# Moving normalisation to ScalarE, an FP4 addition to GpSimd, quantising x in pairs, and giving reads of shared banks top priority

## The chip, the core and the metric

The kernel runs on one core of a Trainium2 chip. The metric is the device time of one execution in microseconds (us). The engines are named as in the profile: PE is TensorE (PEld its weight loads), DVE is VectorE, ACT is ScalarE, POOL is GpSimd, and SP is the engine that issues the DMAs here.

## The reference

The kernel computes two layers on 16 sequences of 512 tokens with 256 channels. The change touches the first one only:

```python
# attention: 16 heads of 16 channels, each turned into a latent of 32
q, k, v = split(x @ c_attn_w.T + c_attn_b)           # in heads
q_lat = rope(q @ q2l_w.T + q2l_b);  k_lat = rope(k @ kv2l_w.T + kv2l_b)
v_lat = v @ kv2l_w.T + kv2l_b
att = softmax(causal((q_lat @ wqk_w.T + wqk_b) @ k_lat.T * 32**-0.5))
y   = (att @ v_lat) @ l2o_w.T + l2o_b
x   = layernorm(x + y @ cproj_w.T + cproj_b)
# feed-forward with FP4 values: blocks of 16 along the last axis
# fp4(t): scale = max|t| of a block / 6, round t/scale to 0, .5, 1, 1.5, 2, 3, 4, 6, times scale
h = silu(fp4(x) @ fp4(w_gate).T) * (fp4(x) @ fp4(w_up).T)   # 704 wide
x = layernorm(x + fp4(h) @ fp4(w_down).T)
# second layer: a recurrence over the 512 tokens, then a gated channel mix
```

## The kernel before

The program has two stages. The first does all of the first layer, one sequence ("batch" `b`) after the other, and stores the result to a DRAM tile `xs`. The second does the recurrence and the channel mix; it begins when the last rows of `xs` are stored, and the change leaves it as it is.

In the first stage the instructions of PE are written out by hand (`tc.manual_schedule` for PE alone), and a scheduler orders those of the other engines by priority, which follows program order unless something raises it. The hand-written order is a list of slots `(b, g, n)`: for each batch, each of four groups `g` of four heads, and each of three sets `n` of score blocks (`BLOCKS`: 512, 384, and 256 + 128 wide). In a slot PE computes the scores of four heads into four PSUM banks (`scores`, L551). DVE adds the mask, takes the row maximum and writes p to SBUF (L563, the maximum in `nm`), which frees the bank. ACT takes the exponential of p (L576), two heads later (`LAG`). One slot later PE transposes p (`turn`, L586) and ACT copies the result out of PSUM (L588, pT). When the three sets of a group are turned, PE multiplies by the values (`weighted`, L617), and `divide` (L631 to L638) divides by the row sums, whose reciprocal POOL spreads out (L602, rcx).

Beside each half slot `Beside` runs tasks from the hand-written list `PLAN`, in its order, paced by the times in `TIME`. A task is named by a letter, the batch counted from the present one, and a part:

- `H`, `V`, `L`: the heads (L383), the values (L366) and the latents of the next groups. For the latents PE multiplies twice (L401), DVE applies cosine and sine (L411, L416), POOL adds both (L417, qc and kc), PE multiplies qc by one more matrix (L420, ps_qf) and ACT copies it out (L422, qr).
- `O`: the output projection of the previous batch (L435). DVE adds the residual x (L441) and takes mean and variance (L89, L90, in mv). POOL makes rstd in two instructions (`rstd_of`: L82 ve, L84 a power). DVE subtracts and multiplies each of four tiles (L448).
- `Q`: queues the FP4 quantisation of one tile of x, 128 tokens by 256 (`fp4`).
- `U`: gate and up projections of one tile. PE transposes the quantised tile (L483, ps_xq), ACT copies it (L485), PE multiplies for both halves of 352 (L493, pg and pu), ACT takes a tanh (L498, th), DVE forms h (L499, L500), and the quantisation of h is queued.
- `D`: the down projection. PE transposes the quantised h (L514, ps_h), ACT copies it (L517 to L519, hT), PE multiplies (L524, ps_d), DVE adds the residual (L527), then `layernorm` as in O but for one tile (L96), and the store to `xs` (L530).

`fp4` is a generator of ten instructions. On DVE: block maximum and scale (L290, L291), inverse (L292, L293), the product x times inverse (L296, q), its power of two (L298), the rounding constant (L299, m), the addition q + m (L302). On POOL: q − m (L303) and the product with the scale (L304, xq or hq). Queued generators are stepped one yield per half slot (`vector_step`), and in full where their result is needed (`vector_done`).

All tiles of PSUM but one come from one pool of seven rotating banks (`mm`), so each PE instruction that opens a bank waits for the engine that read that bank seven tiles ago. The residual x of a batch is loaded at the batch's start (`load_residual`, L355, three buffers), and POOL adds the projection's bias to it (L357).

Of the kernel before, what the change touches and what calls it, by code (L numbers as in the profile page):

```python
# [10 lines left out]
F32 = mybir.dt.float32  # L11
# [46 lines left out]
def tile_kernel(ctx: ExitStack, tc: tile.TileContext, I: dict, out: bass.AP):  # L58
# [33 lines left out]
    def layernorm(dst, src):  # L92
        mv = small.tile([P, 4, 2], F32, tag="mv", name="mv")
        stats_into(mv[:, 0, :], src)
        rs = rstd_of(mv, 1, LN_EPS)
        nc.vector.tensor_scalar(dst, src, mv[:, 0, 0:1], rs[:, 0:1], ALU.subtract, ALU.mult)  # L96
# [42 lines left out]
    with ExitStack() as a:  # L139
# [119 lines left out]
        xres = a.enter_context(tc.tile_pool(name="xres", bufs=3))  # L259
# [7 lines left out]
        def mm(name):  # L267
            return ps_m.tile([P, 512], F32, tag="mm", name=name)

        def fp4(dst, x, nb, rows=P):  # L270

            n = nb * 16
            sc = ffn.tile([P, 44], F32, tag="q_sc", name="q_sc", bufs=2)[:rows, :nb]
            inv = ffn.tile([P, 44], F32, tag="q_inv", name="q_inv", bufs=2)[:rows, :nb]  # L280
            q = ffn.tile([P, FF], F32, tag="q_q", name="q_q", bufs=2)[:rows, :n]
            m = ffn.tile([P, FF], F32, tag="q_m", name="q_m", bufs=2)[:rows, :n]

            def blocks(t):
# [8 lines left out]
            nc.vector.tensor_scalar(inv, inv, 1.0 - 2.0**-23, None, ALU.mult)  # L293
            if n > C:
                yield
            nc.vector.tensor_tensor(blocks(q), blocks(x), over(inv), ALU.mult)  # L296
            yield
            nc.vector.tensor_scalar(m.bitcast(U32), q.bitcast(U32), 0x7F800000, None, ALU.bitwise_and)  # L298
            nc.vector.tensor_scalar(m, m, 1.0, 1.5 * 2.0**22, ALU.max, ALU.mult)  # L299
            if n > C:  # L300
                yield
            nc.vector.tensor_tensor(q, q, m, ALU.add)  # L302
            nc.gpsimd.tensor_tensor(q, q, m, ALU.subtract)  # L303
            nc.gpsimd.tensor_tensor(blocks(dst), blocks(q), over(sc), ALU.mult)  # L304
# [55 lines left out]
        def values(b):  # L360
            v = vpad[b % 2]
            for j in range(0, NT, 2):
                ps = mm("ps_v")
                for i in range(2):
                    for cc in range(2):
                        nc.tensor.matmul(  # L366
                            ps[:, i * C : i * C + C],
                            xT_of[b][:, cc, (j + i) * P : (j + i) * P + P], wv[:, cc, :],
                            start=cc == 0, stop=cc == 1,
                        )  # L370
                for odd in range(2):
                    nc.scalar.copy(
                        v[:, j : j + 2, odd::2, odd * 16 : odd * 16 + 16],
                        ps.rearrange("p (j n o d) -> p j n o d", j=2, o=2, d=16)[:, :, :, odd, :],
                    )
                yield 0.9

        def heads(b):
            hs = heads_of[b] = att.tile([P, 4, T], F32, tag="heads", name="heads")
            for n in range(4):  # L380
                ps = mm("ps_h")
                for cc in range(2):
                    nc.tensor.matmul(  # L383
                        ps, wqk[:, cc, n, :], xT_of[b][:, cc, :], start=cc == 0, stop=cc == 1
                    )
                bias = col("cab", n) if n < 2 else cabk[:, n - 2 : n - 1]
                nc.scalar.activation(hs[:, n, :], ps, AF.Identity, bias=bias)
                yield 1.7

        def latents(b, g):  # L390
# [17 lines left out]
            for k, ps in pair(""):  # L408
                of[k] = att.tile([P, T], F32, tag=f"{k}c", name=f"{k}c", bufs=1 if k == "q" else 3)
                bias = col("q2lb" if k == "q" else "kv2lb")  # L410
                nc.vector.scalar_tensor_tensor(of[k], ps, bias, cos, ALU.add, ALU.mult)  # L411
            yield 0.86
            for k, ps in pair("s"):
                x = att.tile([P, T], F32, tag=f"{k}s", name=f"{k}s")
                bias = q2lbs if k == "q" else col("kv2lbs")
                nc.vector.scalar_tensor_tensor(x, ps, bias, sin, ALU.add, ALU.mult)  # L416
                nc.gpsimd.tensor_tensor(of[k], of[k], x, ALU.add)  # L417
# [4 lines left out]
            nc.scalar.activation(qr, ps, AF.Identity, bias=wqkb)  # L422
# [3 lines left out]
        def out_projection(b):  # L426
# [4 lines left out]
            for j in range(0, NT, 2):  # L431
# [9 lines left out]
                nc.vector.tensor_tensor(both, ps, both, ALU.add)  # L441
# [4 lines left out]
            rs = rstd_of(mv, 4, LN_EPS)  # L446
            for j in range(NT):
                nc.vector.tensor_scalar(  # L448
                    x[:, j, :], x[:, j, :], mv[:, j, 0:1], rs[:, j : j + 1],
                    ALU.subtract, ALU.mult,  # L450
                )
# [21 lines left out]
        def quantize(b, j):  # L473
            xq_of[b, j] = xq = ffn.tile([P, C], F32, tag="xq", name="xq", bufs=2)
            queue(("x", b, j), fp4(xq, x_of[b][:, j, :], C // 16))
            yield 0.0

        def ffn_up(b, j):
            vector_done(("x", b, j))
            xq = xq_of.pop((b, j))  # L480
# [4 lines left out]
            nc.scalar.copy(xqT.rearrange("p c t -> p (c t)"), ps[:, : 2 * P])  # L485
            yield 0.3
            h = ffn.tile([P, FF], F32, tag="h", name="h", bufs=2)
            for f in range(2):
# [9 lines left out]
                nc.scalar.activation(th, pg[:, :352], AF.Tanh, scale=0.5)  # L498
                nc.vector.scalar_tensor_tensor(th, th, 1.0, pg[:, :352], ALU.add, ALU.mult)  # L499
                nc.vector.scalar_tensor_tensor(h[:, fs], th, 0.5, pu[:, :352], ALU.mult, ALU.mult)  # L500
# [5 lines left out]
        def ffn_down(b, j):  # L506
# [10 lines left out]
            nc.scalar.copy(hT[:, 0:4, :].rearrange("p k t -> p (k t)"), pa)  # L517
            nc.scalar.copy(hT[:, 4, :], pb[:, :P])
            nc.scalar.copy(hT[:64, 5, :], pb[:64, P : 2 * P])  # L519
# [7 lines left out]
            nc.vector.tensor_tensor(x, ps[:, :C], x, ALU.add)  # L527
            layernorm(x, x)
# [14 lines left out]
        def scores(b, g, n):  # L543
# [14 lines left out]
            for h in range(4):  # L558
                p = pp.tile([P, T], F32, tag="p", name="p")
                nm = small.tile([P, 2], F32, tag="nm", name="nm", bufs=10)  # L560
                for u, (i, at) in enumerate(BLOCKS[n]):
                    own = slice(at, at + (i + 1) * P)
                    nc.vector.tensor_tensor_reduce(  # L563
                        out=p[:, own], in0=S[h][:, own], in1=mask[:, T - (i + 1) * P :],
# [17 lines left out]
        def turn(n, p):  # L582
# [5 lines left out]
            nc.scalar.copy(pT[:, :w], ps[:, :w])  # L588
# [35 lines left out]
        def divide():  # L624

            for b, g, py, rcx in undivided:
# [6 lines left out]
                nc.scalar.copy(rT.rearrange("p c t -> p (c t)"), ps[:, : 2 * P])  # L633
                to = y_of[b][g % 2 * 64 : g % 2 * 64 + 64, g // 2, :]
                to = to.rearrange("p (i t) -> p i t", t=P)
                for half, blocks in enumerate((slice(0, 4, 3), slice(1, 3))):
                    hs = slice(half * 64, half * 64 + 64)
                    nc.vector.tensor_tensor(to[:, blocks, :], py[hs], rT[hs], ALU.mult)  # L638
# [16 lines left out]
            "L0.1", "U-2.3", "L0.1", "U-2.3", "D-2.2", "L0.1", *["O-1"] * 2, "Q-1.0", "Q-1.1", "D-2.2",  # L655
# [48 lines left out]
        with tc.manual_schedule(engines={mybir.EngineType.PE}):  # L704
            load(0)
            load_residual(0)
# [6 lines left out]
            for slot in slots + [None]:  # L713
                if slot:
                    b, g, n = slot
                    if g == 0 and n == 0:
# [4 lines left out]
                        if b > 0:  # L721
                            load_residual(b)
                        beside = Beside(b)
                        if b == 2:
                            ta, wb, wc, bout = recurrent_weights()
                    tiles = scores(b, g, n)
# [463 lines left out]
```

## Time and profile before

| | |
|---|---|
| time, median of three runs | 2796.65 us (2793.94 to 2797.45) |
| the profiled execution's own time | 2794.07 us |
| its span | 2792.3 us |
| mean granted TensorE clock | 0.972 |
| first stage | to about 2013 us; one batch every 116.7 us when steady |
| busy in the span | PE 2542.9, DVE 1907.0, ACT 1620.5, POOL 1037.7 us |

The span is the time from the first to the last recorded event of the profiled execution. Busy time is summed per engine; the engines work side by side. In the lists of waits a line reads: waiting engine, tile and line, then the engine, tile and line that ended the wait, then total us, times and the longest. In a timeline a line reads: start and duration in us, engine, line, operation, output and inputs, form, count, and in brackets the idle time before it with what ended it.

### The profile page before, as it was taken

What the parts mean: (1) busy time and instruction counts of PE and PEld (TensorE: products, weight loads), DVE (VectorE), ACT (ScalarE), POOL (GpSimd) and SP (SyncE); (2) the same over time, 40 slices, a digit from 0 to 9 for tenths busy, and PEclk for the clock granted to TensorE, in tenths of its full rate; (3) what the DMA queues carried; (4) which work ended last, traced back from release to release, by engine and by line L of the source; (5) the groups of instructions that cost most, each with busy time, mean ns of one, the idle gap of its engine ahead of it and who ended that gap; (6) DMA issues with size and microseconds to landing.
All of it is one profiled execution on the core that took longest, in us unless ns stands there. A gap on an engine that the chain in (4) does not pass through costs nothing. (4 is left out here: it accounts for less than half of the span.)

```text
span 2792.3 us, 73881 instructions
## 1 busy us (share of the span) xinstructions
PE 2542.9 (91%) x28766; PEld 1734.2 (62%) x28766; DVE 1907.0 (68%) x5613; ACT 1620.5 (58%) x5604; POOL 1037.7 (37%) x1617
## 2 busy tenths in 40 slices
PE   6779999999999999999999999987699999999997
PEld 3445565665665666656566656555477777777775
DVE  3666777777777777777777777776636666666655
ACT  2646556665665656656566565654156666666663
POOL 3222323333332323323233232332355555555553
PEclk9879999999999999999999999999889999999999
DMA  3000000000000000000000000000011111111100
GB/s 114 24 6 11 14 13 13 14 20 14 13 12 14 20 9 18 12 14 20 7 20 13 12 14 5 14 5 7 24 34 37 37 37 37 37 37 37 37 26 24
DMA packets 58000, 61.31 MB, mean 22 GB/s; under 512 B 7857, under 2 KB 53041, under 8 KB 57650
## 3 DMA queue, kind: packets, MB, share of 16 engines
q1 hardware_dynamic: 56786, 55.54, 6.4%
q8 instruction: 226, 3.70, 0.5%
q14 instruction: 124, 1.02, 0.1%
q10 hardware_dynamic: 864, 1.05, 0.1%
HBM read 39.79 MB, written 16.78 MB: 20 GB/s over the span
## 5 line engine op out<-in xcount | busy, mean ns | idle before, releaser
L576 ACT ACTIVATE p<-p,nm 128x512 f32<-128x512 f32 (+3 forms) x1024 | 567.7, 558 | 573.7 <-DVE nm L563 571.4
L992 ACT ACTIVATE hist<-u 64x64 f32<-64x64 f32 x2048 | 444.1, 218 | 279.8 <-PE u L984 187.5
L563 DVE CUSTOM_DVE_ANT_0 p<-S,mask 128x512 f32<-128x512 f32 (+3 forms) x1024 | 441.2, 482 | 123.3 <-PE S L551 123.2
L586 PEld LDWEIGHTS ps_pt<-ident,p 128*128 128x128 f32 x2560 | 290.1, 142 | 298.5 <-DVE nm L563 100.1
L303 POOL TENSOR_TENSOR q_q<-q_q,q_m 128x256 f32<-128x256 f32 (+1 forms) x142 | 168.1, 1184 | 781.6 <-DVE q_q L302 758.8
L586 PE MATMUL ps_pt<-ident,p 128*128 128x128 f32 x2560 | 403.7, 284 | 45.4 <-DVE nm L563 37.9
L984 PEld LDWEIGHTS u<-hist,ta 128*64 128x64 f32 x8176 | 360.7, 138 | 123.2 <-ACT hist L992 50.2
L588 ACT COPY pT<-ps_pt 128x384 f32<-128x384 f32 (+1 forms) x768 | 370.3, 511 | 110.4 <-PE ps_pt L586 108.2
L984 PE MATMUL u<-hist,ta 128*64 128x32 f32 x8176 | 391.9, 219 | 11.4 <-ACT hist L992 9.9
L551 PE MATMUL S<-kc,qr 32*128 32x512 f32 (+3 forms) x2048 | 258.5, 478 | 3.1 <-ACT qr L422 0.9
L946 PE MATMUL u<-xt,wb 128*64 128x64 f32 x4128 | 224.9, 231 | 1.0 <-DVE xt L798 0.7
L82 POOL TENSOR_SCALAR ve<-mv 128x1 f32<-128x1 f32 (+2 forms) x144 | 28.4, 197 | 501.6 <-DVE mv L90 497.9
L576 ACT ACTIVATION_READ_ACCUMULATOR p<-p,nm 128x1 f32 x1024 | 196.9, 192 | 0.0
L524 PE MATMUL ps_d<-wdT,hT 128*128 128x256 f32 (+1 forms) x768 | 192.9, 393 | 2.3 <-ACT hT L517 1.3
L493 PE MATMUL pg<-wgT,xqT 128*128 128x352 f32 x512 | 182.0, 479 | 5.8 <-ACT xqT L485 5.7
L493 PE MATMUL pu<-wuT,xqT 128*128 128x352 f32 x512 | 175.6, 466 | 1.4 <-DVE nm L563 1.4
L946 PEld LDWEIGHTS u<-xt,wb 128*64 128x64 f32 x4128 | 166.6, 140 | 6.7 <-DVE xt L798 1.0
L551 PEld LDWEIGHTS S<-kc,qr 32*128 32x128 f32 x2048 | 122.7, 187 | 75.9 <-issue 36.1
L617 PE MATMUL py<-pT,vpad 128*32 128x128 f32 x5120 | 162.1, 279 | 3.4 <-ACT pT L588 3.4
L524 PEld LDWEIGHTS ps_d<-wdT,hT 128*128 128x128 f32 (+1 forms) x768 | 137.4, 192 | 43.2 <-issue 21.4
L617 PEld LDWEIGHTS py<-pT,vpad 128*32 128x32 f32 x5120 | 140.9, 112 | 36.4 <-issue 27.4
L417 POOL TENSOR_TENSOR qc<-qc,qs 128x512 f32<-128x512 f32 x64 | 81.6, 1275 | 212.0 <-DVE qs L416 211.9
(163 smaller groups left out, 4601.2 us busy)
## 6 DMA issues: line engine op xcount, KB each, us to landing
xT<-in_xT_dram SPq DMA_DIRECT2D x16, 512.0 KB
x<-in_x_dram SPq DMA_DIRECT2D x16, 512.0 KB
xs<-x SPq DMA_DIRECT2D x64, 128.0 KB
x<-xs SPq DMA_DIRECT2D x32, 256.0 KB
xm<-xs SPq DMA_DIRECT2D x32, 256.0 KB
out_dram<-o SPq DMA_DIRECT2D x64, 128.0 KB
caw<-in_caw_dram SPq DMA_DIRECT2D x1, 768.0 KB
w<-in_w_down_dram SPq DMA_DIRECT2D x2, 352.0 KB
```

What stands on the lines that cost most here:

```text
L303: nc.gpsimd.tensor_tensor(q, q, m, ALU.subtract)
L493: nc.tensor.matmul(dst[:, :352], xqT[:, cc, :], w[:, cc, fs], start=cc == 0, stop=cc == 1)
L524: nc.tensor.matmul(ps[:, :C], hT[:n, kb, :], wdT[:n, kb, :], start=kb == 0, stop=kb == NFB - 1)
L551: nc.tensor.matmul(S[h][:, at : at + w], q[rs, i * P : i * P + P], k[rs, :w], start=True, stop=True,)
L563: nc.vector.tensor_tensor_reduce(out=p[:, own], in0=S[h][:, own], in1=mask[:, T - (i + 1) * P :], scale=1.0, scalar=-MASKED, op0=ALU.add, ...
L576: nc.scalar.activation(p[:, own], p[:, own], AF.Exp, bias=nm[:, u : u + 1], scale=-1.0, accum_out=sum_of[b, g][:, cb, half, h : h + 1],)
L586: nc.tensor.transpose(ps[:, at : at + P], p[:, at : at + P], ident)
L588: nc.scalar.copy(pT[:, :w], ps[:, :w])
L617: nc.tensor.matmul(py[q * 32 : q * 32 + 32, PLACE[i][1], :], vpad[b % 2][:, j, g * 4 + h, :], pt, start=j == 0 and h % 2 == 0, stop=j == i ...
L946: nc.tensor.matmul(u[rs, k, par:n:2, bs : bs + 16], wb[:, g * 2 + k, par, half, rs], xt[:, g, at : at + n - par : 2, :], start=par == 0 an ...
L984: nc.tensor.matmul(into[cs, :, c, :], ta[:, t % 2, g * 2 + k, cs], own[:, :, c, :], start=False, stop=True, skip_group_check=True,)
L992: nc.scalar.activation(state[g][rs, :, r * 32 : r * 32 + 32].rearrange("p k (s b) -> p k s b", s=2), u[rs, :, t - t0, :] .rearrange("p k ( ...
```

## The change

Five things are changed, all in the first stage.

1. `soon` wraps an instruction in `tc.high_priority()`. It is put around the ACT and DVE instructions that read PSUM banks (and the two additions of L417 on POOL). The exponentials, which read SBUF, keep their ordinary priority.
2. Normalisation goes from DVE to ACT. POOL computes, after rstd, off = −mean × rstd in two more small instructions, and ACT applies x × rstd + off as one Identity activation for each tile (`normal`).
3. In `fp4`, the addition q + m goes from DVE to POOL where the row is longer than 512, that is for h and w_down (704).
4. x is quantised two tiles at a time, as rows of 512; `PLAN` loses Q-1.1 and Q-1.3, and the `xq` tiles are twice as long.
5. The residual is loaded at the batch's last group (`g == 3`) and has two buffers.

```diff
-    def layernorm(dst, src):
-        mv = small.tile([P, 4, 2], F32, tag="mv", name="mv")
-        stats_into(mv[:, 0, :], src)
-        rs = rstd_of(mv, 1, LN_EPS)
-        nc.vector.tensor_scalar(dst, src, mv[:, 0, 0:1], rs[:, 0:1], ALU.subtract, ALU.mult)
+    def normal(xs, mv):
+        n = len(xs)
+        rs = rstd_of(mv, n, LN_EPS)
+        off = small.tile([P, 4], F32, tag="off", name="off")
+        nc.gpsimd.tensor_tensor(off[:, :n], mv[:, :n, 0], rs[:, :n], ALU.mult)
+        nc.gpsimd.tensor_scalar(off[:, :n], off[:, :n], -1.0, None, ALU.mult)
+        for i, x in enumerate(xs):
+            nc.scalar.activation(
+                x, x, AF.Identity, bias=off[:, i : i + 1], scale=rs[:, i : i + 1]
+            )
...
-        xres = a.enter_context(tc.tile_pool(name="xres", bufs=3))
+        xres = a.enter_context(tc.tile_pool(name="xres", bufs=2))
...
+        def soon(op, *args, **kw):
+            with tc.high_priority():
+                op(*args, **kw)
...
             nc.vector.tensor_scalar(m, m, 1.0, 1.5 * 2.0**22, ALU.max, ALU.mult)
-            if n > C:
+            if n > 2 * C:
+                nc.gpsimd.tensor_tensor(q, q, m, ALU.add)
+            else:
                 yield
-            nc.vector.tensor_tensor(q, q, m, ALU.add)
+                nc.vector.tensor_tensor(q, q, m, ALU.add)
             nc.gpsimd.tensor_tensor(q, q, m, ALU.subtract)
             nc.gpsimd.tensor_tensor(blocks(dst), blocks(q), over(sc), ALU.mult)
...
-                nc.vector.scalar_tensor_tensor(x, ps, bias, sin, ALU.add, ALU.mult)
-                nc.gpsimd.tensor_tensor(of[k], of[k], x, ALU.add)
+                soon(nc.vector.scalar_tensor_tensor, x, ps, bias, sin, ALU.add, ALU.mult)
+                soon(nc.gpsimd.tensor_tensor, of[k], of[k], x, ALU.add)
...
-            rs = rstd_of(mv, 4, LN_EPS)
-            for j in range(NT):
-                nc.vector.tensor_scalar(
-                    x[:, j, :], x[:, j, :], mv[:, j, 0:1], rs[:, j : j + 1],
-                    ALU.subtract, ALU.mult,
-                )
+            normal([x[:, j, :] for j in range(NT)], mv)
...
         def quantize(b, j):
-            xq_of[b, j] = xq = ffn.tile([P, C], F32, tag="xq", name="xq", bufs=2)
-            queue(("x", b, j), fp4(xq, x_of[b][:, j, :], C // 16))
+            xq_of[b, j] = xq = ffn.tile([P, 2 * C], F32, tag="xq", name="xq", bufs=2)
+            both = x_of[b][:, j : j + 2, :].rearrange("p j c -> p (j c)")
+            queue(("x", b, j), fp4(xq, both, C // 8))
             yield 0.0
 
         def ffn_up(b, j):
-            vector_done(("x", b, j))
-            xq = xq_of.pop((b, j))
+            vector_done(("x", b, j // 2 * 2))
+            xq = xq_of[b, j // 2 * 2][:, j % 2 * C : j % 2 * C + C]
...
-                nc.scalar.activation(th, pg[:, :352], AF.Tanh, scale=0.5)
-                nc.vector.scalar_tensor_tensor(th, th, 1.0, pg[:, :352], ALU.add, ALU.mult)
-                nc.vector.scalar_tensor_tensor(h[:, fs], th, 0.5, pu[:, :352], ALU.mult, ALU.mult)
+                soon(nc.scalar.activation, th, pg[:, :352], AF.Tanh, scale=0.5)
+                soon(nc.vector.scalar_tensor_tensor, th, th, 1.0, pg[:, :352], ALU.add, ALU.mult)
+                soon(nc.vector.scalar_tensor_tensor, h[:, fs], th, 0.5, pu[:, :352], ALU.mult, ALU.mult)
...
-            layernorm(x, x)
+            mv = small.tile([P, 4, 2], F32, tag="mv", name="mv")
+            stats_into(mv[:, 0, :], x)
+            normal([x], mv)
...
         PLAN = [
-            "L0.1", "U-2.3", "L0.1", "U-2.3", "D-2.2", "L0.1", *["O-1"] * 2, "Q-1.0", "Q-1.1", "D-2.2",
+            "L0.1", "U-2.3", "L0.1", "U-2.3", "D-2.2", "L0.1", *["O-1"] * 2, "Q-1.0", "D-2.2",
             "L0.2", "V1", "L0.2", "V1", "D-2.3", "U-1.0", "L0.2", "Q-1.2", "U-1.0",
-            "L0.3", "D-2.3", "L0.3", "U-1.0", "U-1.1", "L0.3", "H1", "Q-1.3", "H1", "U-1.1", "H1",
+            "L0.3", "D-2.3", "L0.3", "U-1.0", "U-1.1", "L0.3", "H1", "H1", "U-1.1", "H1",
...
-            load_residual(0)
...
-                        if b > 0:
-                            load_residual(b)
                         beside = Beside(b)
...
+                    if g == 3 and n == 0:
+                        load_residual(b)
                     tiles = scores(b, g, n)
```

The other places where `soon` is added are the remaining reads of PSUM named above: the copies of the values and heads (L372, L387), L411, L422, the addition of L441, L485, L517 to L519, L527, L563, L588, L633 and L638.

More of the change, by code (lines that the diff above doesn't have):

```diff
@@ L371, in values @@
                 for odd in range(2):
-                    nc.scalar.copy(
+                    soon(
+                        nc.scalar.copy,
                         v[:, j : j + 2, odd::2, odd * 16 : odd * 16 + 16],
@@ L386, in heads @@
                 bias = col("cab", n) if n < 2 else cabk[:, n - 2 : n - 1]
-                nc.scalar.activation(hs[:, n, :], ps, AF.Identity, bias=bias)
+                soon(nc.scalar.activation, hs[:, n, :], ps, AF.Identity, bias=bias)
                 yield 1.7
@@ L410, in latents @@
                 bias = col("q2lb" if k == "q" else "kv2lb")
-                nc.vector.scalar_tensor_tensor(of[k], ps, bias, cos, ALU.add, ALU.mult)
+                soon(nc.vector.scalar_tensor_tensor, of[k], ps, bias, cos, ALU.add, ALU.mult)
             yield 0.86
@@ L421, in latents @@
             qr = att.tile([P, T], F32, tag="qr", name="qr", bufs=3)
-            nc.scalar.activation(qr, ps, AF.Identity, bias=wqkb)
+            soon(nc.scalar.activation, qr, ps, AF.Identity, bias=wqkb)
             stack_of[b, g] = qr, of["k"]
@@ L440, in out_projection @@
                 both = x[:, j : j + 2, :].rearrange("p j c -> p (j c)")
-                nc.vector.tensor_tensor(both, ps, both, ALU.add)
+                soon(nc.vector.tensor_tensor, both, ps, both, ALU.add)
                 for i in range(j, j + 2):
@@ L484, in ffn_up @@
             xqT = ffn.tile([P, 2, P], F32, tag="xqT", name="xqT", bufs=2)
-            nc.scalar.copy(xqT.rearrange("p c t -> p (c t)"), ps[:, : 2 * P])
+            soon(nc.scalar.copy, xqT.rearrange("p c t -> p (c t)"), ps[:, : 2 * P])
             yield 0.3
@@ L516, in ffn_down @@
                 )
-            nc.scalar.copy(hT[:, 0:4, :].rearrange("p k t -> p (k t)"), pa)
-            nc.scalar.copy(hT[:, 4, :], pb[:, :P])
-            nc.scalar.copy(hT[:64, 5, :], pb[:64, P : 2 * P])
+            soon(nc.scalar.copy, hT[:, 0:4, :].rearrange("p k t -> p (k t)"), pa)
+            soon(nc.scalar.copy, hT[:, 4, :], pb[:, :P])
+            soon(nc.scalar.copy, hT[:64, 5, :], pb[:64, P : 2 * P])
             yield 0.7
@@ L526, in ffn_down @@
                 )
-            nc.vector.tensor_tensor(x, ps[:, :C], x, ALU.add)
-            layernorm(x, x)
+            soon(nc.vector.tensor_tensor, x, ps[:, :C], x, ALU.add)
+            mv = small.tile([P, 4, 2], F32, tag="mv", name="mv")
+            stats_into(mv[:, 0, :], x)
+            normal([x], mv)
             at_row = xs.rearrange("(t b) c -> b t c", b=B)
@@ L562, in scores @@
                     own = slice(at, at + (i + 1) * P)
-                    nc.vector.tensor_tensor_reduce(
-                        out=p[:, own], in0=S[h][:, own], in1=mask[:, T - (i + 1) * P :],
+                    soon(
+                        nc.vector.tensor_tensor_reduce, out=p[:, own], in0=S[h][:, own], in1=mask[:, T - (i + 1) * P :],
                         scale=1.0, scalar=-MASKED, op0=ALU.add, op1=ALU.min,
@@ L587, in turn @@
             pT = ptp.tile([P, T], F32, tag="pT", name="pT")
-            nc.scalar.copy(pT[:, :w], ps[:, :w])
+            soon(nc.scalar.copy, pT[:, :w], ps[:, :w])
             return pT
@@ L632, in divide @@
                 rT = att.tile([P, 2, P], F32, tag="rT", name="rT")
-                nc.scalar.copy(rT.rearrange("p c t -> p (c t)"), ps[:, : 2 * P])
+                soon(nc.scalar.copy, rT.rearrange("p c t -> p (c t)"), ps[:, : 2 * P])
                 to = y_of[b][g % 2 * 64 : g % 2 * 64 + 64, g // 2, :]
@@ L637, in divide @@
                     hs = slice(half * 64, half * 64 + 64)
-                    nc.vector.tensor_tensor(to[:, blocks, :], py[hs], rT[hs], ALU.mult)
+                    soon(nc.vector.tensor_tensor, to[:, blocks, :], py[hs], rT[hs], ALU.mult)
                 if g == 3:
```

## The prediction

> **What bounds the kernel now.** I read the page's busy line first, then a table of windows, then the waits of the steady stretch, then the timeline at the places that those waits name.
>
> ```profile
> PE 2542.9 (91%) x28766; PEld 1734.2 (62%) x28766; DVE 1907.0 (68%) x5613; ACT 1620.5 (58%) x5604; POOL 1037.7 (37%) x1617
> ```
> ```profile
> 640.00:1200.00 560.00, 530.74 (x4050) 338.08 (x4049) 426.69 (x1283) 342.53 (x1036) 175.42 (x206) 1.00 0.05 15
> 1960.00:2030.00 70.00, 43.60 (x195) 29.61 (x195) 41.76 (x90) 8.11 (x23) 27.35 (x35) 0.82 0.09 28
> ```
>
> The columns of the windows are length, then busy PE, PE loads, DVE, ACT, POOL, then clock. The attention stage (to about 2013 us) repeats every 116.7 us, once per batch. Between 640 and 1200 PE is busy 95%, DVE 76%, ACT 61%, POOL 31%. TensorE is the bound and no other engine is near full, so averages decide nothing: a part of the change matters where PE waits for it. The chain of waits covers only the time after about 2090 us, so for this stage I use the waits from 400 to 1800 us (12 batches; columns: total us, times, longest).
>
> ```profile
> PE ps_pt L586 <- DVE nm L563: 28.6, 34, 1.2
> PE ps_v L366 <- DVE nm L563: 10.6, 12, 0.9
> PE ps_qf L420 <- DVE q_inv L293: 10.2, 12, 0.9
> DVE x L96 <- POOL rstd L84: 51.3, 36, 2.4
> DVE x L448 <- POOL rstd L84: 17.1, 12, 1.4
> ```
>
> PE's listed waits come to 64 us, 5.3 per batch. DVE stands blocked for 68.4 us behind POOL's rstd. These two are linked, as the timeline of one such place (call it site 1) shows:
>
> ```profile
> 519.76 1.69 POOL L303 TENSOR_TENSOR q_q<-q_q,q_m 128x704 f32<-128x704 f32 x1 [17.30 <-DVE q_q L302]
> 521.81 1.39 POOL L304 TENSOR_TENSOR hq<-q_q,q_sc 128x704 f32<-128x704 f32 x1
> 523.15 0.55 POOL L84 TENSOR_TENSOR rstd<-ve,neg_half 128x1 f32<-128x1 f32 x1
> 523.74 0.46 DVE L96 TENSOR_SCALAR x<-x,mv,rstd 128x256 f32<-128x256 f32 x1 [2.37 <-POOL rstd L84]
> 524.86 1.16 PE L586 MATMUL ps_pt<-ident,p 128*128 128x128 f32 x6 [1.16 <-DVE nm L563]
> 524.90 0.72 ACT L576 ACTIVATE p<-p,nm 128x512 f32<-128x512 f32 x1 [2.63 <-DVE nm L563]
> 526.33 0.46 ACT L588 COPY pT<-ps_pt 128x384 f32<-128x384 f32 x1
> 526.68 0.46 ACT L498 ACTIVATE th<-pg 128x352 f32<-128x352 f32 x1
> ```
>
> DVE stands 2.37 us at the normalisation, the maximum L563 behind it is late, PE waits 1.16 us for the bank that L563 reads, and ACT idles 2.63.
>
> [...] So a normalisation moved to ScalarE takes its wait along. [...] beside POOL's L303 and L304 at 940.5 to 943.7, the 256-wide L298 and L299 took 1.66 and 1.43 us, against 0.29 alone.
>
> **The change, part by part.** Set beside each other, the two built programs have the same PE order. On ACT and DVE a few reads move by one or two places: the priorities alone (soon) are worth about nothing, since the reads already stood near where PE frees them. What moves is the work.
>
> Per batch DVE loses eight normalisations at 0.42 (3.3 us), four adds of 704 at 0.886 (3.5), and about 7 us where four x quantisations become two: 14 of 90 us. ACT gains eight of about 0.5 us (4 us; it is 61% busy). POOL gains four adds of 704 (6.8 at 1.71, the row of its subtraction) and two small instructions, about 0.25 each, per normalisation group. None of these sums is itself on the path; now the places.
>
> Site 1. DVE is no longer blocked. But ACT's new order is one exponential, the normalisation, three exponentials, pT, th. POOL first adds (1.71, from DVE's L299 ending at 518.6: 520.3), then ve (0.2), subtraction (1.7: 522.2), rstd (0.55), hq (1.39: 524.2), and only then the two offset instructions: 524.7. ACT, free at 521.2, stands 3.5 us, normalises to 525.2, does three exponentials at 0.72 and reaches pT at about 527.4 against 526.33. Behind it th feeds DVE's L499 and L500, which free the banks of PE's second gate product. PE gains the 1.16 us and loses it again there. Ends: 0 to +1.6; I take **+1.3**.
>
> O (attention output). L448 waits 1.43 us for rstd and takes 1.38, with L563 behind it. After, L563 runs 2.5 us sooner, while ACT's exponentials start about 1 us later (ACT waits for the offsets and then does four normalisations). Two PE stalls of 0.4 to 0.5 us lie there: −0.6 to 0, **−0.3**.
>
> Q (quantising x):
>
> ```profile
> 908.48 0.40 POOL L602 COPY rcx<-rc 128x256 f32<-128x256 f32 x1
> 909.88 1.27 POOL L417 TENSOR_TENSOR qc<-qc,qs 128x512 f32<-128x512 f32 x1 [1.00 <-DVE qs L416]
> 911.20 1.12 PE L420 MATMUL ps_qf<-qc,w 128*128 128x512 f32 x2 [0.85 <-DVE q_inv L293]
> ```
>
> PE's L420 waits for qc (the release at 911.15 is POOL's; the wait names DVE). Before qc POOL did two x tiles of 256: four instructions of about 0.7. After, both pairs stand ahead of qc: two subtractions and two products of 512, by the slope between the 256 and 704 rows 1.29 and 1.07, so 4.7, with rcx 0.40, qc 1.27 and gaps of 0.08 some 6.8 us from the first add, which itself ends some 0.9 later (906.4). qc is done at 913.2 to 913.8 instead of 911.15, and PE already stands waiting. Ends +1.5 to +2.65; **+2.3**.
>
> The other D places. At 925 ACT stands until 926.9 and is then busy without a gap (+0.25); at 955.7 PE waits 0.99 us behind the quantisation of h, from which DVE loses an add (−0.2). **0 in sum**, −0.3 to +0.4. The addition of 704 on POOL delays hq by 0.8 to 1 us; PE uses hq some 10 us later or more (962.4 against 972.8), so it costs nothing but POOL's delay at site 1. The residual load, issued on SP's queue in the batch's last quarter instead of at its start, now waits for the store of the batch before (two buffers, not three) and passes no store that is waited for; POOL's adds behind it stand up to 4 us, where POOL has no other work due, and are needed a batch later: nothing.
>
> Steady sum 1.3 − 0.3 + 2.3 + 0 = **+3.3 per batch** (0.6 to 4.6); about 14 batches behave so: +46 (8 to 65).
>
> The ends. From 1935 to 2026 the last batch runs O, Q, U, D one after another with nothing beside it (PE busy 43.6 of 70 us), and PE waits 15.7 us for hq and 6.0 for xq directly. There the addition on POOL costs 0.8 for each of four exposed hq, the pair about 2 before the first xq, and the last normalisation about 0.9 more: less what DVE saves, **+5** (2 to 10). At the start x's additions come later and two weight additions go to POOL: **+1** (−3 to +4). The recurrence after it is untouched.
>
> Sum +52 on the profiled execution's 2794.07: 2846; the median of the runs stands 2.6 above it: **2849**. Own range of this case: 2804 to 2876.
>
> **Rivals.**
>
> *VectorE's relief wins: faster.* If ACT has slack for its waits, the PE waits on DVE's nm go: 28.6 + 10.6 and two of 3.1 and 2.6, 44.9 us in 12 batches, 52 in 14; with +6 for the ends the time is about 2750. For it: DVE loses 14 of 90 us and ACT is 61% busy. Against: the wait for POOL moves, it does not vanish. It decides if offsets are ready within some 2 us of ACT's arrival and qc comes no later than now. Chance 0.20.
>
> *Only one place bites.* Site 1 alone gives 1.3 − 0.3 = 1.0 per batch, Q alone 2.0: 2817 to 2831. Chance 0.20.
>
> *The change does not do what it says.* The orders hardly move and gains equal losses: 2797. For it: PE's order is the same. Chance 0.10, of which 0.06 lie within 0.2% (5.6 us, about what a measurement here can tell from no change), the rest split.
>
> The forecast has 0.50.
>
> **How the numbers follow.** Faster 0.20 + 0.02, same 0.06, slower 0.50 + 0.20 + 0.02. The range of 8 in 10 takes in the bounds of the forecast, the single places and the near half of the faster case: 2770 to 2880.
>
> **What would show it.** Right: DVE no longer waits on rstd; ACT's normalisation shows about 3.5 us of wait on POOL at site 1; ps_qf waits over 2 us more; PE's waits at ps_pt on DVE shrink; steady batches last about 120 us. Wrong: the ACT normalisation waits under 1.5 us, qc ready as early as now, or batches at or under 116.7 us. If the batch grows without these two waits, my mechanism is wrong even if the time is right.

## The result and the profile after

The changed kernel takes 2896.59 us (median of four runs, 2890.76 to 2912.31) against 2797.05 for the kernel before in the same set: 1.0363 times as long, interval 1.0317 to 1.0408. Slower was forecast, at 2849 with 2880 as the upper end; the loss is 99.5 us where 52 were summed.

The page's busy line of the changed kernel, and the stretch 640 to 1200 us from its windows (length; busy PE, PE loads, DVE, ACT, POOL; clock, DMA share, GB/s):

```profile
PE 2599.9 (90%) x28766; PEld 1762.1 (61%) x28766; DVE 1749.8 (61%) x5163; ACT 1678.2 (58%) x5732; POOL 1159.9 (40%) x1779
```
```profile
640.00:1200.00 560.00, 520.50 (x3831) 329.39 (x3830) 355.62 (x1084) 339.51 (x1015) 200.22 (x236) 0.97 0.04 13
```

VectorE's busy time fell by 157 us and bought nothing. Two columns matter: PE did 3831 matmuls in the stretch instead of 4050, and its clock column reads 0.97 instead of 1.00. That second number was not in the prediction. A steady batch takes 122.9 us instead of 117.0 (the mean of 11 batches; most of those before take 116.5 to 117).

PE's waits from 400 to 1800 us (total us, times, longest). Many lines are now L279, the helper `soon`:

```profile
PE ps_qf L434 <- POOL qc L279: 28.0, 11, 2.5
PE ps_pt L599 <- ACT pT L279: 13.8, 23, 2.5
PE ps_xq L494 <- DVE qs L279: 12.4, 11, 1.1
PE ps_pt L599 <- DVE nm L279: 8.5, 11, 0.8
```

The wait of ps_pt on DVE fell from 28.6 to 8.5 us; a longer one on POOL's qc and a new one on ACT's pT stand beside it.

**Site 1**, from the timelines of POOL, ACT and PE:

```profile
650.69 1.68 POOL L312 TENSOR_TENSOR q_q<-q_q,q_m 128x704 f32<-128x704 f32 x1 [16.77 <-DVE q_m L310]
652.72 1.68 POOL L316 TENSOR_TENSOR q_q<-q_q,q_m 128x704 f32<-128x704 f32 x1
654.90 1.39 POOL L317 TENSOR_TENSOR hq<-q_q,q_sc 128x704 f32<-128x704 f32 x1
656.52 0.23 POOL L98 TENSOR_SCALAR off<-off 128x1 f32<-128x1 f32 x1
656.78 0.60 ACT L100 ACTIVATE x<-x,off,rstd 128x256 f32<-128x256 f32 x1 [3.51 <-POOL off L98]
659.91 0.55 PE L599 MATMUL ps_pt<-ident,p 128*128 128x128 f32 x3 [0.82 <-ACT pT L279]
```

The offsets come behind three POOL steps of 704, ACT stands 3.51 us, and its pT is late for PE.

**Q**, from the timelines of DVE, POOL and PE:

```profile
691.18 1.03 DVE L310 TENSOR_SCALAR q_m<-q_m 128x512 f32<-128x512 f32 x1
692.24 0.69 DVE L315 TENSOR_TENSOR q_q<-q_q,q_m 128x512 f32<-128x512 f32 x1
692.86 0.74 DVE L279 SCALAR_TENSOR_TENSOR qs<-ps_qs,q2lbs,sin 128x512 f32<-128x512 f32 x1
693.02 1.28 POOL L316 TENSOR_TENSOR q_q<-q_q,q_m 128x512 f32<-128x512 f32 x1 [1.09 <-DVE q_q L315]
694.37 1.06 POOL L317 TENSOR_TENSOR xq<-q_q,q_sc 128x512 f32<-128x512 f32 x1
695.39 1.26 POOL L279 TENSOR_TENSOR qc<-qc,qs 128x512 f32<-128x512 f32 x1
696.70 2.08 PE L434 MATMUL ps_qf<-qc,w 128*128 128x512 f32 x2 [2.54 <-POOL qc L279]
```

The second pair runs ahead of qs on DVE and ahead of qc on POOL, and PE waits 2.54 us. The last line holds the other half of the story: two matmuls that took 1.12 us before take 2.08. The windows of 3.41 us around it show why:

```profile
692.95:696.36 3.41, 0.41 (x2) 0.20 (x2) 1.31 (x2) 2.12 (x8) 3.27 (x3) 1.00 0.00 0
696.36:699.78 3.42, 3.08 (x6) 1.71 (x7) 0.00 (x0) 0.97 (x2) 1.51 (x2) 0.50 0.00 0
```

PE did 0.41 us of work in the first, and in the whole of the second its clock is 0.50. From 400 to 1800 us the kernel before has 3 such half-clock spells (3.41, 3.41 and 6.83 us, 13.7 in all), the changed one 23 (each 3.41 us, 78.5 in all), about two in a batch. In each of these two traces the starts of all spells lie on one grid of 3.4133 us, to within 0.01 us; a step below is one interval of that grid.

Only one of the two follows a stall. The other comes at the start of a batch, from 651.98 in this one:

```profile
649.00 2.84 PE L564 MATMUL S<-kc,qr 32*128 32x512 f32 x8
```
```profile
648.57:651.98 3.41, 3.30 (x13) 1.47 (x13) 3.14 (x15) 3.41 (x14) 1.29 (x1) 1.00 0.01 2
651.98:655.39 3.41, 3.41 (x9) 1.48 (x8) 2.79 (x9) 1.29 (x6) 3.25 (x5) 0.50 0.00 0
```

In the step ahead of it PE is busy for 3.30 of 3.41 us, but mostly with the batch's first scores, which use 32 of the 128 rows. So this spell came without an idle step ahead of it. What goes with it here is where the grid falls. In the 24 batches that start from 400 to 1800 us in the two traces, half clock followed in all 13 in which a step began 0.12 to 0.58 us before the first scores, and in none of the other 11, where one began 0.03 us before them (one batch) or 0.71 to 3.15 us. The changed batch lasts 36.0 steps (122.9 us), so the grid meets the scores at nearly the same place every time, and 11 of 12 batches have the spell. The batch before lasts 34.3 (117.0 us), the place drifts, and 2 of 12 have it. In all, 12 of the 23 spells of the changed kernel follow a step in which PE was busy 96% or more.

**Where a batch's time goes.** I took 11 steady batches of each trace and went through PE's matmuls: from one start to the next, less 0.84 ns a column (the pace of back-to-back matmuls here, 0.43 us for 512). What is over is counted as half clock, up to half of its overlap with a spell; the rest, where over 0.12 us, as a wait; all else is the base. This is bookkeeping: a wait inside a spell can be booked as half clock. The times before are medians, and the other columns come from one execution each, which lies up to 16 us from its kernel's median (e17).

| kernel | times before | batch us | waits | half clock | base |
|---|---|---|---|---|---|
| before | 1 | 117.0 | 8.9 | 0.5 | 107.7 |
| changed | 1.036 | 122.9 | 10.8 | 3.4 | 108.8 |
| e1 x single | 1.018 | 119.8 | 8.7 | 2.7 | 108.4 |
| e2 norm on DVE | 1.019 | 119.5 | 11.0 | 0.0 | 108.5 |
| e3 addition on DVE | 1.040 | 123.8 | 10.9 | 4.3 | 108.6 |
| e4 fill at qf | 1.036 | 122.9 | 10.6 | 1.7 | 110.6 |
| e5 both fills | 1.034 | 121.7 | 7.9 | 1.2 | 112.5 |
| e6 priorities + addition | 1.015 | 119.5 | 10.6 | 0.9 | 108.0 |
| e7 pairs alone | 1.006 | 117.4 | 8.4 | 0.6 | 108.3 |
| e8 norm alone | 1.018 | 119.5 | 9.9 | 1.7 | 107.9 |
| e9 rstd first | 1.003 | 117.5 | 9.0 | 1.1 | 107.4 |
| e10 addition alone | 1.012 | 118.9 | 9.9 | 1.5 | 107.4 |
| e11 priorities alone | 1.010 | 118.1 | 8.7 | 1.7 | 107.7 |
| e12 no priorities | 1.034 | 122.9 | 11.9 | 3.5 | 107.5 |
| e13 changed, swap | 1.029 | 122.1 | 9.8 | 3.2 | 109.0 |
| e14 before, swap | 1.015 | 119.6 | 9.9 | 1.8 | 107.9 |
| e15 e11 with a fill | 1.022 | 120.7 | 9.0 | 1.7 | 110.1 |
| e16 pad, 128 rows | 1.038 | 123.4 | 8.6 | 0.3 | 114.5 |
| e17 pad, 32 rows | 1.067 | 129.7 | 8.6 | 6.6 | 114.5 |

The changed batch is 5.9 us longer: 1.9 in waits, 1.1 in the base (small gaps and drawn-out instructions below the bound), 2.9 in half clock.

### The profile page after: what moved, and what is told of

The parts are those of the page before. It is cut to its first block, busy times and chain, and to the rows that moved or that the text cites. A ratio compares the mean times of both kernels' runs of the same rounds, so it can differ in the third digit from the quotient of the medians.

```text
span 2890.9 us, 73842 instructions
## 1 busy us (share of the span) xinstructions
PE 2599.9 (90%) x28766; PEld 1762.1 (61%) x28766; DVE 1749.8 (61%) x5163; ACT 1678.2 (58%) x5732; POOL 1159.9 (40%) x1779
## 5 line engine op out<-in xcount | busy, mean ns | idle before, releaser
L279 DVE CUSTOM_DVE_ANT_0 p<-S,mask 128x512 f32<-128x512 f32 (+3 forms) x1024 | 439.7, 482 | 154.5 <-PE S L564 154.3
L599 PEld LDWEIGHTS ps_pt<-ident,p 128*128 128x128 f32 x2560 | 296.2, 144 | 298.9 <-issue 111.7
L279 ACT COPY pT<-ps_pt 128x384 f32<-128x384 f32 (+1 forms) x768 | 366.8, 509 | 58.6 <-PE ps_pt L599 56.6
L312 POOL TENSOR_TENSOR q_q<-q_q,q_m 128x704 f32<-128x704 f32 x66 | 110.8, 1678 | 617.1 <-DVE q_m L310 593.5
L564 PE MATMUL S<-kc,qr 32*128 32x512 f32 (+3 forms) x2048 | 267.0, 478 | 4.7 <-DVE th L279 1.6
L279 DVE SCALAR_TENSOR_TENSOR th<-th,pg 128x352 f32<-128x352 f32 x128 | 66.7, 521 | 322.9 <-ACT th L279 321.7
L504 PE MATMUL pg<-wgT,xqT 128*128 128x352 f32 x512 | 191.3, 499 | 11.7 <-ACT xqT L279 6.3
L316 POOL TENSOR_TENSOR q_q<-q_q,q_m 128x704 f32<-128x704 f32 (+2 forms) x110 | 160.6, 1460 | 77.7 <-DVE q_q L315 72.6
L100 ACT ACTIVATE x<-x,off,rstd 128x256 f32<-128x256 f32 x128 | 73.1, 597 | 202.6 <-POOL off L98 180.3
L630 PE MATMUL py<-pT,vpad 128*32 128x128 f32 x5120 | 171.3, 284 | 5.6 <-ACT pT L279 5.5
```

What stands on the lines that cost most here:

```text
L279: op(*args, **kw)
L504: nc.tensor.matmul(dst[:, :352], xqT[:, cc, :], w[:, cc, fs], start=cc == 0, stop=cc == 1)
L564: nc.tensor.matmul(S[h][:, at : at + w], q[rs, i * P : i * P + P], k[rs, :w], start=True, stop=True,)
L599: nc.tensor.transpose(ps[:, at : at + P], p[:, at : at + P], ident)
L630: nc.tensor.matmul(py[q * 32 : q * 32 + 32, PLACE[i][1], :], vpad[b % 2][:, j, g * 4 + h, :], pt, start=j == 0 and h % 2 == 0, stop=j == i ...
```

## The experiments

Theory S+C, with which the runs were planned: PE stalls behind whoever stands in line after POOL's long steps, and half-clock spells follow the stalls and cost by themselves.

**Undoing one part.** e1: x one tile at a time, with its Q tasks.

```diff
-            xq_of[b, j] = xq = ffn.tile([P, 2 * C], F32, tag="xq", name="xq", bufs=2)
...
+            xq_of[b, j] = xq = ffn.tile([P, C], F32, tag="xq", name="xq", bufs=2)
+            queue(("x", b, j), fp4(xq, x_of[b][:, j, :], C // 16))
...
```

> The changed kernel with x quantised one tile at a time again (its order of Q tasks too); the rest as changed. Theory S+C (stalls of PE plus the half-clock spells that follow a stalled window): the wait of PE at ps_qf goes from 2.5 us back to about 1, and the half-clock spell right behind it goes, so the batch falls from 122.9 us by 2.7 + 1.7 to about 118.5 and the time from 2893 by 14 x 4.4 to about 2832. Rival N (ACT blocked by the normalisation is the cause, the x pair only a small part): at most 1 us a batch, 2880. Rival P (POOL's additional work in sum is the cause): 2880 or more, since POOL's total hardly changes.

2843.91 us, 1.0185 (1.0169 to 1.0200). The wait at ps_qf is gone, as S+C says, and with it half of the loss; the batch is 119.8, not 118.5, because spells appear at other places (2.7 us of half clock is left).

e2: normalisation on VectorE, in `normal`.

```diff
-        off = small.tile([P, 4], F32, tag="off", name="off")
...
-            nc.scalar.activation(
-                x, x, AF.Identity, bias=off[:, i : i + 1], scale=rs[:, i : i + 1]
-            )
+            nc.vector.tensor_scalar(
+                x, x, mv[:, i, 0:1], rs[:, i : i + 1], ALU.subtract, ALU.mult
+            )
```

> The changed kernel with the normalisation back on VectorE (subtract and multiply, no offset instructions on GpSimd). Theory S+C: PE's stall at ps_qf and its spell stay; the place of the last down projection and of the output projection change by 1 us or less a batch: 2870 to 2895. Rival N: most of the loss goes, 2800 to 2830. Rival P: the POOL chain before the normalisation is as long as before plus the addition, so VectorE is now blocked longer than in the kernel before: 2890 to 2920.

2846.96 us, 1.0188 (1.0168 to 1.0209): no theory's range, and the stall at ps_qf, which S+C had staying, fell from 2.5 to 1.2 us. It is the best pair with the changed kernel in the table: waits 11.0 and 10.8, base 108.5 and 108.8, half clock 0.0 and 3.4, batch 119.5 and 122.9. With as much waiting in all, what differs is the clock. The pair is not a pure test, since the places of the waits differ too.

e3: the 704-wide addition back on VectorE.

```diff
-            if n > 2 * C:
-                nc.gpsimd.tensor_tensor(q, q, m, ALU.add)
-            else:
+            if n > C:
                 yield
-                nc.vector.tensor_tensor(q, q, m, ALU.add)
+            nc.vector.tensor_tensor(q, q, m, ALU.add)
```

> The changed kernel with the FP4 addition of the 704-wide rows back on VectorE. Theory S+C: offsets are ready 1.7 us sooner, so ACT waits 1.8 instead of 3.5 us at the last down projection, PE regains about 1.3 us a batch there and the tail about 3: 2870 (2860 to 2885). Rival P: half of the loss or more, 2800 to 2845. Rival N: about 2870 too, since the wait of ACT is halved.

2904.82 us, 1.0400 (1.0383 to 1.0417), no faster than the changed kernel: both ranges missed. POOL and ACT at site 1:

```profile
660.29 1.69 POOL L314 TENSOR_TENSOR q_q<-q_q,q_m 128x704 f32<-128x704 f32 x1 [17.89 <-DVE q_q L313]
664.20 0.40 POOL L613 COPY rcx<-rc 128x256 f32<-128x256 f32 x1
664.83 0.23 POOL L98 TENSOR_SCALAR off<-off 128x1 f32<-128x1 f32 x1
665.10 0.60 ACT L100 ACTIVATE x<-x,off,rstd 128x256 f32<-128x256 f32 x1 [3.36 <-POOL off L98]
```

One POOL step of 1.7 us is gone, yet ACT waits 3.36 instead of 3.51. The scheduler put rcx ahead of the offsets, and the chain starts later: 2.8 us after the batch's scores begin (PE's L562 at 657.47), where in the changed kernel POOL's addition started 1.7 us after them (649.00).

**Fills.** e4 and e5 put extra products into PE's waits.

```diff
+            for _ in range(2 if g == 2 else 0):
+                nc.tensor.matmul(ps, w1, cos, start=True, stop=True)
             nc.tensor.matmul(ps, w1, of["q"], start=True, stop=True)
```

> The changed kernel with two extra products (w1 by the cosine table, 512 columns) written by PE into the bank of ps_qf ahead of the product that waits for qc, in the third group of each batch only; the real product overwrites them, so the result is as before. They fill PE's wait of 2.5 us with about 1.9 us of work and leave all other engines alone. Theory S+C: the half-clock spell behind that wait goes although the product starts no sooner: 14 x 1.7 = 24 us less, about 2869 (2855 to 2880), mean clock about 0.965. Rival (the half-clock spells cost nothing, since other engines pace PE there): 2893 or slower, with the mean clock up all the same.

2892.94 us, 1.0357 (1.0336 to 1.0377): the time is that of the changed kernel, though one spell a batch is gone. The expected 24 us did not come: the fill is 1.8 us of work, and PE's wait at ps_pt for pT grew from 13.8 to 32.0 us in the twelve batches, with the one spell now behind it. The spell at the scores is gone as well: PE comes to pT sooner and waits longer. So half clock was taken out and no time came back, as the rival has it.

> The changed kernel with the two extra products ahead of ps_qf in the third group (as in e4) and two more of them ahead of ps_q in the second group (into the bank that the real product then overwrites), where PE later waits 1.5 to 3 us for ACT's pT behind the normalisation. In e4 one half-clock spell a batch was left, just behind that second place. Theory S+C: no regular spell is left, the clock rises to about 0.97 and the batch falls from 122.9 by up to 1.7 us to 121.2 or so: 2870 (2855 to 2882). Rival F (the spells are free, the batch is paced by ACT and POOL): 122.9 us a batch and 2885 or more, with the clock up all the same.

The second fill is the same loop ahead of ps_q in the second group. 2888.27 us, 1.0338 (1.0298 to 1.0379); the batch fell to 121.7 although 3.7 us were added to its base. The time lies in rival F's range (2885 or more); the batch lies between the two theories, nearer to the 121.2 of S+C.

**One part alone.** e6 to e8 and e10 to e12 are put together from the hunks of the change and their reverses; all keep the later residual load with two buffers. No run has that load alone, so what it costs is not known, and is part of each result here.

> The changed kernel with both x single and the normalisation on VectorE: what is left of the change are the priorities, the addition of the 704-wide rows on GpSimd and the later residual load. Theory S+C: the two sources of stalls are gone, and e3 showed the addition on GpSimd to be worth some 12 us: the kernel before or a little faster, 2780 to 2797. Rival A (the parts cost what they cost alone, 49 and 46 us): 2893 - 95 = 2798. Rival L (priorities or the later load have their own price): 2805 or more.

2838.93 us, 1.0154 (1.0126 to 1.0183). S+C and the sum of parts both missed; rival L's range holds it, and e10 and e11 below show a price of each of the two parts. VectorE, which normalises here, stands behind the addition on POOL, and pu waits for its nm (21.0 us in the twelve batches).

> The kernel before with x quantised in pairs alone (and the later residual load with two buffers, without which the longer tiles do not fit); no priorities, normalisation and addition on VectorE. Theory S+C: qc is late behind two subtractions and two products of 512, PE waits over 2 us at ps_qf and a half-clock spell follows: +2.0 to +4.4 us a batch, 2820 to 2853. Rival I (the pair hurts only together with the normalisation on ScalarE): 2785 to 2797, since VectorE saves 7 us a batch.

2812.61 us, 1.0065 (1.0049 to 1.0080), in neither range, and the batch is 117.4: the pair alone does not make the stall. DVE and POOL at Q:

```profile
678.62 0.65 DVE L275 SCALAR_TENSOR_TENSOR qs<-ps_qs,q2lbs,sin 128x512 f32<-128x512 f32 x1
679.34 1.27 POOL L275 TENSOR_TENSOR qc<-qc,qs 128x512 f32<-128x512 f32 x1 [0.25 <-DVE q_inv L300]
683.84 1.27 POOL L310 TENSOR_TENSOR q_q<-q_q,q_m 128x512 f32<-128x512 f32 x1 [1.55 <-DVE q_q L309]
```

Here qs and qc come before the second pair's last steps. It is with the normalisation on ScalarE that the second pair gets ahead of them. PE's wait at ps_qf in e2, e3 and e12 (below), in this order:

```profile
PE ps_qf L431 <- POOL qc L276: 14.8, 12, 1.2
PE ps_qf L432 <- POOL qc L279: 28.0, 11, 2.5
PE ps_qf L433 <- POOL qc L278: 20.9, 11, 2.5
```

e2 has all of the change but this normalisation, and its second pair stays behind qc. e3 lacks the addition on POOL and e12 the priorities, and in both the second pair stands ahead of qc as in the changed kernel. So the stall takes the pair and the normalisation together, as rival I said of the pair. This fits with e1 and e2, which undo one of the two each and come from 1.036 to 1.018 and 1.019, while e6, which undoes both, comes to 1.015, hardly lower. Why the scheduler's order depends on the normalisation is open.

> The kernel before with the normalisation on ScalarE alone (and the later residual load): no priorities, x single, addition on VectorE. Theory S+C: ACT waits some 3 us for the offsets at the last down projection, PE then at ps_pt for pT, and half-clock spells follow in about one window a batch: +2 to +4 us a batch, 2820 to 2850. Rival V (VectorE's relief wins when the rest is as before): 2780 or less.

2843.55 us, 1.0184 (1.0160 to 1.0207), in the range of S+C: PE waits 29.3 us in the twelve batches at ps_pt behind ACT's pT. There is about one spell a batch in the mean, but only 5 of the 13 follow a step with that wait. The other 8 follow steps with scores 512 wide in which PE is busy 95% or more, so the spells are not what S+C says.

> The kernel before with the 704-wide FP4 addition on GpSimd alone (and the later residual load). Theory S+C: VectorE, which normalises here, now stands behind two steps of 1.7 us on POOL instead of one at the last down projection, some 1.5 us longer, and L563 and PE behind it: about as e6, 118.5 to 119.5 us a batch, 2820 to 2840. Rival P0 (in e6 it was the priorities that cost): 2785 to 2797.

2829.28 us, 1.0124 (1.0104 to 1.0143), in the range of S+C: DVE's wait for rstd rises from 68.4 us in 12 batches (both lines of before) to 77.1. The longest grows by 0.8 us (2.4 to 3.2), where 1.5 was expected.

> The kernel before with the priorities alone (and the later residual load): nothing moved between engines, x single. As predicted from the orders, which hardly differ: 2788 to 2798. Rival P0 (the priorities alone make what e6 lost): 2820 to 2840.

2819.29 us, 1.0097 (1.0073 to 1.0121): slower, against the prediction. The waits did not grow (8.7 against 8.9), but they are bunched:

```profile
PE ps_pt L592 <- DVE nm L276: 28.5, 34, 1.2
PE ps_v L374 <- DVE nm L276: 20.4, 12, 1.7
```

ps_v waits 20.4 us instead of 10.6, ps_q and ps_qs less; there are 11 spells in the twelve batches where before had 3, and half clock grew by 1.2 us, the batch by 1.1.

> The changed kernel without the priorities; all moved work as changed. Theory S+C: the stalls come from work that stands before what is waited for on POOL and ACT, the priorities are worth little: 2880 to 2900. Rival P0: 2850 or less. Rival G (the priorities are what keeps the reads early when work is moved, so the change without them is worse): 2910 or more.

2888.38 us, 1.0335 (1.0319 to 1.0351): with the work moved, the priorities make no difference that these runs separate.

**A repair that failed.** e9 puts `with tc.high_priority():` around the two instructions of `rstd_of` in the kernel before.

> The kernel before with one edit: GpSimd's two rstd instructions are issued under high priority, so that at the last down projection of a batch its order is subtraction, ve, rstd, product instead of subtraction, ve, product, rstd. Theory S+C (what costs is the engine that stands in line behind POOL's long FP4 steps): VectorE's wait for rstd there falls from 2.4 to about 1.0 us, PE's wait of 1.2 us at ps_pt behind it goes, the product hq is 0.7 us later, which nobody waits for: about 1.2 us a batch, 2793 - 17 = 2776 (2768 to 2786). Rival (another wait takes its place, PE is held by ACT's exponentials there anyway): 2788 to 2797.

2804.12 us, 1.0031 (1.0018 to 1.0043). POOL, DVE and PE at site 1:

```profile
638.59 0.55 POOL L85 TENSOR_TENSOR rstd<-ve,neg_half 128x1 f32<-128x1 f32 x1
639.11 1.38 POOL L305 TENSOR_TENSOR hq<-q_q,q_sc 128x704 f32<-128x704 f32 x1
639.18 1.47 DVE L97 TENSOR_SCALAR x<-x,mv,rstd 128x256 f32<-128x256 f32 x1 [2.02 <-POOL rstd L85]
641.30 1.45 PE L494 MATMUL pu<-wuT,xqT 128*128 128x352 f32 x4 [0.36 <-DVE nm L564]
```

rstd is ready sooner, but the normalisation now runs beside POOL's long product and takes 1.47 us instead of 0.46: wait and work together 3.5 us against 2.8. The normalisation ends 0.16 us after POOL's product. The prediction has two more DVE steps that took longer beside POOL's L303 and L304, 1.66 and 1.43 us against 0.29 alone; what makes them longer is not shown.

**Moving PE's own work.** e13 and e14 swap two entries of `PLAN`.

```diff
-            ... "U-1.0", "L0.2", "Q-1.2", "U-1.0",
+            ... "U-1.0", "Q-1.2", "U-1.0", "L0.2",
```

> The changed kernel with one swap in the hand-written order of PE: the step U-1.0 that does the first gate and up products comes before the third step of L0.2 (ps_qf) instead of after it, so PE has 2.4 us of work of its own while qc is late. Nothing is added or removed. Theory S+C: the wait of 2.6 us at ps_qf goes, a shorter one of up to 1 us for ACT's xqT comes in its place, and the half-clock spell behind it goes: 1.6 to 3.4 us a batch less, 2848 to 2872. Rival F (batch paced by ACT and POOL): 2885 or more.

2875.5 us, 1.0291 (1.0261 to 1.0321), just outside the range of S+C. The wait at ps_qf is gone (2.6 us a batch), but waits for xqT (1.0) and pT (1.0 more) took its place, and 3.2 us of half clock are left.

> The kernel before with the same swap. Theory S+C: its wait at ps_qf (1.3 us a batch) goes, a wait for xqT of some 0.6 comes: 0.5 to 0.7 us a batch, 2786 (2780 to 2792), unless the new order makes a window of little PE work, which a half-clock spell then follows: 2800 to 2815. Rival F: 2795 as before.

2832.34 us, 1.0146 (1.0128 to 1.0164): worse, and beyond even the case with a new spell. Right behind its transposes, the gate product now waits for ACT:

```profile
PE pg L493 <- ACT xqT L485: 24.4, 12, 2.0
```

That is 2.0 us a batch where 0.6 was expected, and a spell in each batch.

> The kernel of e11 (priorities alone: as many stalls as before, but one half-clock spell a batch instead of 0.2) with one extra product of 512 columns, overwritten by the real one, ahead of ps_ks in the third group, 0.9 us of work put ahead of PE's wait of 1.8 us at ps_v. Theory S+C: the spells that follow that wait go (half of them or more) and the wait itself takes the added work in: 0.4 to 1.2 us a batch less, 2804 to 2814 against 2819. Rival F (the spells cost nothing): 2819 or more, with fewer spells all the same.

The fill is one product ahead of ps_ks. 2854.87 us, 1.0225 (1.0206 to 1.0244): a miss. It made ks late and moved the wait instead of taking it in:

```profile
PE ps_qf L431 <- DVE ks L276: 34.2, 12, 2.9
```

**The price of half clock by itself.** Up to e15 no edit had changed the clock and left the waits where they were. e16 and e17 do: eight extra products in the kernel before, which differ in the rows that they use.

```diff
                     ps = mm(f"ps_{k}{turned}")
+                    for _ in range(8 if (g, k, turned) == (3, "q", "") else 0):
+                        nc.tensor.matmul(ps, w1[:128, :], cos[:128, :], start=True, stop=True)
```

e17 has 32 in the place of both 128.

> The kernel before with eight extra products of 512 columns on PE in the last group of each batch (128 rows by 128), into the bank of ps_q, which the real product then overwrites. Both theories: about 7 us of PE work more in each of 16 batches, less what its waits take in: 2793 + 16 x 5 to 7 = 2875 to 2905, with as few half-clock spells as before or fewer.

> The same kernel as e16 but with the eight extra products on 32 of the 128 rows: the same instructions, columns and waits, a quarter of the array at work. Theory S+C [...]: a spell follows in every batch and PE takes 1.0 to 1.7 us longer over what comes then, so 16 to 27 us more than e16. Rival F (the half clock only shows where PE waits anyhow, and is free): the same time as e16 within 0.2%, with or without more spells.

2896.12 us, 1.0384 (1.0365 to 1.0404), and 2979.04 us, 1.0666 (1.0630 to 1.0702). The stretch 640 to 1200 us, e16 and then e17:

```profile
640.00:1200.00 560.00, 533.42 (x3918) 335.23 (x3917) 402.39 (x1218) 323.57 (x982) 164.75 (x193) 1.00 0.04 13
```
```profile
640.00:1200.00 560.00, 536.20 (x3794) 329.93 (x3793) 385.64 (x1149) 310.59 (x937) 159.01 (x185) 0.95 0.04 14
```

PE is as busy in both, but did 124 matmuls fewer at a clock of 0.95. At a clock of 1.00 the extra products follow each other every 0.43 us on 32 rows as on 128, so the rows by themselves cost nothing here. Waits are 8.6 us a batch in both, the base 114.5 in both; half clock is 0.3 and 6.6, the batch 123.4 and 129.7. In this kernel the half clock costs by itself, and the rival that it is free falls here. The size was under-estimated (83 us, not 16 to 27): a spell lasted 6.8 or 10.2 us at the padding and another 3.4 or 6.8 followed at site 1, 13.3 us a batch where 3.4 was reckoned with.

What the changed kernel would gain without its 3.4 us of half clock is not shown by this: e4 took 1.7 of them out and e5 2.2, and the batch fell by 0 and by 1.2 us.

None of the versions beats the kernel before; e9 comes nearest.

## Why the prediction was right or wrong

The direction and the two main waits were right; the sum lacked a term.

- **Site 1.** Right in mechanism: ACT was to stand 3.5 us and stood 3.51. The 0.5 us for one normalisation on ACT was an estimate; L100 took 0.60. PE's own balance can't be read off in the changed kernel: the spell at the scores holds PE back ahead of the same wait, and where it is gone (e4) the wait for pT is 1.5 us a batch longer.
- **Q.** Right: +2.3 was taken; ps_qf went from 1.0 to 2.6 us a batch and ps_xq from 0.3 to 1.2, +2.5. But it is no property of the pair: e7 shows that the order makes it, and e2, e3 and e12 that the order comes with the pair and the normalisation on ScalarE together.
- **Steady sum.** Waits and base grew by 3.0 us a batch where 3.3 was summed. That is near in part by luck: Q took 2.5, all other waits together fell by 0.6 where 1.0 was to be added, and the base, which the prediction did not price, rose by 1.1.
- **The step that failed** is "Steady sum ... = +3.3 per batch": it adds up PE's waits and lets PE run at full clock all the time. Half clock, by the table, rose from 0.5 to 3.4 us a batch, and this 2.9 was taken as zero. About half of it follows the stall at Q. The other half follows the scores, where PE does not stall, in the batches in which a step began 0.12 to 0.58 us before them. That half clock costs time by itself is shown in the kernel before (e16, e17: 2896 and 2979 us); how much of the 2.9 is a net loss in the changed kernel stays open (e4, e5). The window line of before even showed the clock column at 1.00, and the tail's at 0.82, where PE is busy 43.6 of 70 us; I read neither as a price.
- **Priorities.** "Worth about nothing" was wrong for them alone (with the later load): 1.0% (e11). The waits bunched at ps_v, and 6 of the 11 spells come right behind them; that this is the cause is not shown, as e15 missed. In the changed kernel no difference shows (e12).
- **The addition on POOL** was to cost only its delay at site 1. It costs 1.2% alone (e10, with the later load), where VectorE stands behind it, and nothing that shows in the changed kernel (e3).
- **The ends.** Of the 98.6 us between the two traced spans, −2.5 lie before the third batch (+1 was taken), 79.2 in the thirteen that follow (46 was taken for fourteen), 18.5 in the rest of the first stage, of which the last batch's own 6 leaves some 12 where +5 was taken, and 3.4 in the second stage (0 was taken).

The rival "VectorE's relief wins" failed at the point named for it: the offsets were not ready within 2 us of ACT's arrival.

## What to carry to other kernels

Read the clock column beside the busy shares: in the changed kernel a stall of 2.54 us was followed by 3.41 us at a clock of 0.50, and so were scores on 32 of 128 rows with PE busy for 3.30 of 3.41 us. Set the place of such spells in the loop beside its period: with batches of 122.9 us the spell at the scores came in 11 of 12, with batches of 117.0 us in 2 of 12. Relieving an engine that does not bound changes the order that a scheduler makes, and what it pulls forward may stand ahead of what PE waits for: look at the order at the waited-for instruction, not at the sums. Two parts of a change can make a stall that neither makes alone. An operation moved to another engine can take its wait along: here ACT stood 3.51 us at site 1, where VectorE had stood 2.37.

## What was not expected of the hardware

- Half clock came without an idle PE. Two windows of e17, the first full of the 32-row products:

```profile
616.85:620.26 3.41, 3.41 (x9) 1.48 (x8) 0.84 (x2) 1.93 (x7) 0.00 (x0) 1.00 0.00 0
620.26:623.67 3.41, 3.41 (x5) 1.33 (x4) 0.00 (x0) 0.00 (x0) 0.00 (x0) 0.51 0.00 0
```

  PE is busy throughout the first, and its clock is 0.51 in the second all the same. In e16, with the same products on 128 rows, the stretch 640 to 1200 us has a clock of 1.00. How little work on PE a spell follows is not shown: no run varies it between these two.
- Eight batches of the table are close to a whole multiple of 3.4133 us: 35.0 (e2, e6, e8, e14), 36.0 (changed, e4, e12) and 38.0 (e17). The other eleven kernels lie between, the one before at 34.3. Whether batches settle on multiples is open; no run here tests it.
- The start of the second stage has half clock too: before, 13.65 us from 2018.03 and 6.83 from 2065.81; in the changed kernel 17.07 from 2109.49, 6.83 from 2160.69 and 3.41 from 2211.89, all at 0.50. From its first matmul (at 2025.9 and 2121.1) to the end of the span the second stage takes 766.4 and 769.8 us, though its code is the same. That the clock is the cause is not shown.
